# Row-by-row products of a matrix: GpSimd's early input batch moved behind the first load, and small loads added after the last store

## The chip, the cores and the metric

The kernel runs on one core of one Trainium2 chip. The metric is the device time of the launch in microseconds; lower is better.

## The reference

The input is a float32 matrix of 4096 rows and 256 columns. For each row the kernel must give all products of two of its elements, the upper triangle with the diagonal, 256 x 257 / 2 = 32,896 numbers a row:

```
dot = jnp.einsum('bi,bj->bij', inputs, inputs)
iu, ju = jnp.triu_indices(256)
return dot[:, iu, ju]
```

The input has 4.2 MB, the output 539 MB. There are no sums: one multiplication for each output element.

## The kernel before

**Tiling.** The 4096 rows are laid over 128 partitions, 32 rows each. A partition works on two rows at a time (REPEAT = 2), a group; sixteen groups make the kernel. The triangle of a group is cut into three pieces of about 10,960 columns (PIECES = 3), and each piece is built in one of two buffers in SBUF (`places`, printed as `o`), which are used in turn. As soon as a piece is built, SP stores it: 128 x 2 x 10,944 (or 11,008) float32, some 11 MB in one DMA. So there are 48 pieces, and the first of them goes out in five smaller stores (the columns in FIRST), so that the stream of stores begins early.

**Who multiplies.** In the loop each piece is shared by VectorE (DVE), which takes the longer runs of the triangle, and GpSimd (POOL), which takes the tail of the piece. Both read a copy of the group, `xv` in SBUF; DVE reads its other operand from `xp`, a copy in PSUM. The first two pieces are made ahead of the loop: piece 0 by DVE and ScalarE (ACT), reading the loaded input `x` itself until DVE has made `xp`, from the fourth part on (DIRECT = 3), and piece 1 (HELPED = 1) by DVE, ACT and GpSimd. GpSimd's share of piece 1 is the tail that an estimate in `tail` puts within HELP microseconds.

**Order.** The order is written out by hand with semaphores. `v_done`, `a_done` and `g_done` tell SP that the parts of a piece are there; `free` tells the engines that a buffer's store has landed; `go` passes that on from DVE to GpSimd. `head` counts the five stores of piece 0. `x_copied` tells DVE that GpSimd has made `xv`.

**Inputs.** SP loads three blocks at the start (NEAR): the first group, with the semaphore `loaded[0]`, then two more blocks. GpSimd issues the rest on its own queue in two batches: an early one (EARLY) at the start, and a late one (LATE) in the third pass of the loop (WHEN = 2). The early batch is a comb: COMB loads, each of every COMB-th row of partitions (`teeth` rows), then one of the `rest` rows. Between the loads stand small transfers, `mark`, that copy a few words of some rows into a buffer that nobody reads. The engines wait for all of these (`far`, `marked`) where they enter the loop.

**What the change touches.** The constants HELP, COMB and MARK; the main body where the early batch is issued (`mark(0, FORE)` and the loop after it) and where GpSimd waits for `loaded[0]`; the first product in `vector` that reads `xp`; the start of `gpsimd`; and the end of `sync`, after the last store. At its end SP takes back the semaphores that are still up: `x_read`, the three of `loaded`, and the two of `free`, which are up when the last stores have landed.

Of the kernel before, what the change touches and what calls it, by code (L numbers as in the profile page):

```python
# [8 lines left out]
F32 = mybir.dt.float32  # L9
# [3 lines left out]
P = 128  # L13
# [7 lines left out]
WHEN = 2  # L21
BEGUN, HAD = 2, 5
HELPED = 1
HELP = 15.0
COMB = 9
FORE, AFT = 5, 14
TENS, FIVES, SKIP = 100, 25, 2
MARK = 64
PLACES = 2
SETS = 5  # L30
PASS = 6
# [104 lines left out]
def kernel(  # L136
# [15 lines left out]
    nc = tc.nc  # L152
# [15 lines left out]
    edge = pool.tile([P, EDGE], F32, name="edge")  # L168
    places = [pool.tile([P, REPEAT, slot], F32, name=f"o{k}") for k in range(PLACES)]
    xt = pool.tile([P, passes, rounds * each], F32, name="x")  # L170
    xv = pool.tile([P, each + 1], F32, name="xv")
    marks = pool.tile([P, 2, 2 * MARK], F32, name="marks")

# [6 lines left out]
    free = [semaphore(f"free{k}") for k in range(PLACES)]  # L180
    head, v_done, a_done, go = (semaphore(s) for s in ("head", "v_done", "a_done", "go"))
    loaded = [semaphore(f"loaded{k}") for k in range(len(NEAR))]
    far, marked = semaphore("far"), semaphore("marked")
    teeth = P // COMB
    rest = P - COMB * teeth

# [38 lines left out]
    def vector(h, pieces: range, ahead: bool, done: int = 0) -> int:  # L225
        for p in pieces:
            place, copied = places[p % PLACES], None
            parts = blocks(p, ahead)
            if ahead and p == 0:
                for c, (_, _, _, block, lo) in enumerate(parts):  # L230
                    if c == DIRECT:
                        nc.vector.tensor_copy(xp, x_of(h, 0)).then_inc(v_own, 1)  # L232
                        done += 1
                        copied = done
                    for i, j, at, length in block:
                        ins = nc.vector.tensor_tensor(  # L236
                            place[:, :, at - lo : at - lo + length],
                            window(x_of(h, 0)[:, j:], [[d, REPEAT], [1, 1], [1, length]]),
                            window(xp[:, i:] if c >= DIRECT else x_of(h, 0)[:, i:], [[d, REPEAT], [1, 1], [0, length]]),
                            ALU.mult,  # L240
                        )
                        if copied:
                            ins._wait_ge(v_own, copied)
                            copied = None
                    ins.then_inc(v_done, 1)
                continue
            if ahead and p == HELPED:
                take(nc.vector, x_copied, 1)
            if not ahead and p % PIECES == 0:
                take(nc.vector, x_read, 1)  # L250
                for to in (xv[:, :each], xp):
                    ins = nc.vector.tensor_copy(to, x_of(h, p // PIECES))  # L252
                    if done:
                        ins._wait_ge(v_own, done)
                    ins.then_inc(v_own, 1)
                    done += 1
                copied = done
            if not ahead:
                if use(p) < uses:
                    nc.vector.wait_ge(free[p % PLACES], 16 * use(p)).then_inc(go, 1)  # L260
                else:
                    take(nc.vector, free[p % PLACES], 16 * uses)
                    nc.vector.sem_inc(go, 1)  # L263
            for _, _, _, block, lo in parts:
                order = interleave(block)

                own = (p + 1) % PIECES == 0 or p == pieces[-1]
                waits = schedule(order)
                counted = {*waits.values(), *([len(order) - 1] if own else [])}
                number = {k: done + 1 + c for c, k in enumerate(sorted(counted))}  # L270
                for k, ((i, j, at, length), m, _) in enumerate(order):
                    at -= lo
                    ins = nc.vector.tensor_tensor(  # L273
                        place[:, :, at : at + m * length],
                        window(xv[:, j:], [[d, REPEAT], [1, m], [1, length]]),
                        window(xp[:, i:], [[d, REPEAT], [1, m], [0, length]]),
                        ALU.mult,
                    )
                    if copied:
                        ins._wait_ge(v_own, copied)  # L280
                        copied = None
                    elif k in waits:
                        ins._wait_ge(v_own, number[waits[k]])
                    if k in counted:
                        ins.then_inc(v_own, 1)
                done += len(counted)
                if own:
                    nc.vector.wait_ge(v_own, done).then_inc(v_done, 1)
                else:
                    ins.then_inc(v_done, 1)  # L290
        return done
# [45 lines left out]
    def gpsimd(h, pieces: range, ahead: bool):  # L337

        done = turns = 0
        if ahead:  # L340
            nc.gpsimd.memset(xv[:, each:], 0.0).then_inc(g_own, 1)  # L341
            nc.gpsimd.tensor_copy(xv[:, :each], x_of(0, 0)).then_inc(g_own, 1)  # L342
            done += 2
            nc.gpsimd.wait_ge(g_own, done).then_inc(x_copied, 1)
        for p in [HELPED] if ahead else pieces:
            place = places[p % PLACES]
            block, lo = helped(p) if ahead else next((block, lo) for _, _, block, _, lo in blocks(p, False))
            turns += not ahead
            last = (p + 1) % PIECES == 0
            order = interleave(block)  # L350
            waits = schedule(order)
            counted = {*waits.values(), *([len(order) - 1] if last else [])}
            number = {k: done + 1 + c for c, k in enumerate(sorted(counted))}
            for k, ((i, j, at, length), m, _) in enumerate(order):
                at -= lo
                ins = nc.gpsimd.tensor_tensor(  # L356
                    place[:, :, at : at + m * length],
                    window(xv[:, j:], [[d, REPEAT], [1, m], [1, length]]),
                    window(xv[:, i:], [[d, REPEAT], [1, m], [0, length]]),
                    ALU.mult,  # L360
                )
                if k == 0 and not ahead:
                    ins._wait_ge(go, turns)
                elif k in waits:
                    ins._wait_ge(g_own, number[waits[k]])
                if k in counted:
                    ins.then_inc(g_own, 1)
            done += len(counted)
            if last:
                nc.gpsimd.wait_ge(g_own, done).then_inc(g_done, 1)  # L370
            else:
                ins.then_inc(g_done, 1)
            if p in (BEGUN, HAD) and not ahead:
                late(h, p)
            if last:
                nc.gpsimd.sem_inc(x_read, 1)
        nc.gpsimd.sem_inc(g_own, -done)
        if turns:
            nc.gpsimd.sem_inc(go, -turns)  # L379

    def sync():
        parts_done = done = joined = 0
        for turn in range(passes * PASS):
            h, p = divmod(turn, PASS)
            ahead, place = turn < AHEAD, places[p % PLACES]
            parts = list(blocks(p, ahead))
            if not ahead or p == HELPED:
                joined += 1
            for lo, hi, *_, base in parts:
                done += 1  # L390
                parts_done += ahead
                nc.sync.wait_ge(v_done, done)
                if ahead and p == HELPED:
                    nc.sync.wait_ge(g_done, joined)
                to = x_out[h, p // PIECES, :, :, base + lo : base + hi]
                store = nc.sync.dma_start(to, place[:, :, lo:hi])
                store._wait_ge(*((a_done, parts_done) if ahead else (g_done, joined)))
                store.then_inc(free[p % PLACES] if len(parts) == 1 else head, 16)
        for sem, count in ((v_done, done), (a_done, parts_done), (g_done, joined)):
            nc.sync.sem_inc(sem, -count)  # L400

# [32 lines left out]
    for engine in (nc.vector, nc.scalar):  # L434
        engine.wait_ge(loaded[0], 16)
    mark(0, FORE)
    for k in range(COMB + 1):
        load(EARLY, slice(k, k + COMB * (teeth - 1) + 1, COMB) if k < COMB else slice(P - rest, P))
        mark(FORE + rest * k, FORE + rest * k + (rest if k < COMB else AFT))
    nc.gpsimd.wait_ge(loaded[0], 16)  # L440

    take(nc.tensor, head, 16 * (len(FIRST) + 1))
    nc.tensor.sem_inc(free[0], 16)
# [2 lines left out]
        all_pieces(engine, pieces_of)  # L446
    sync()
    take(nc.sync, x_read, 1)
    for sem in loaded:
        take(nc.sync, sem, 16)  # L450
    for k in range(PLACES):
# [28 lines left out]
```

## Time and profile before

| what | value |
|---|---|
| time, median of 3 runs | 1263.46 us (1263.3 to 1263.96) |
| time of the profiled execution | 1263.19 us |
| its span in the profile | 1261.4 us |
| busy share of DVE, ACT, POOL | 63%, 2%, 64% |
| moved by DMA | 543.26 MB, mean 431 GB/s |
| share of the 16 DMA engines: SP's queue q1, GpSimd's queue q0 | 99.2%, 0.6% |
| stores of a whole piece, from issue to landing | 31.4 to 33.6 us |
| first products of DVE and ACT | 4.22 us |
| GpSimd's 21 early transfers issued | 1.61 to 13.60 us |
| GpSimd's products of piece 1 | 14.52 to 28.36 us |
| last store issued by SP | 1228.57 us |

The span runs from the first to the last instruction in the profile; the time of the same execution is 1.8 us longer. Times inside the profile count from the span's start. q1 and q0 are rings on the same sixteen DMA engines. The share of a queue is the time that its packets took, over the span of all sixteen.

### The profile page before, as it was taken

The page shows a single profiled execution, that of the slowest core. Times are in us where ns is not written, and L with a number is a line of the kernel's source. Part 1 is how long each engine was busy: PE and PEld are TensorE (multiplying, and loading weights), DVE is VectorE, ACT ScalarE, POOL GpSimd, SP SyncE. Part 2 cuts the span into 40 slices and gives each one's busy share as a digit, 9 for nine tenths or more (in the row PEclk, how much of TensorE's full clock was granted, in tenths as well). Part 3 has the DMA queues.
Part 4 walks back from the last instruction along what each step waited for, and adds up shares of the span by engine and source line. Part 5 has one row for each costly group of instructions (what it writes and reads, how often), then busy time and mean ns, then how long its engine had stood idle before and what let it go on. Part 6 is the DMA issues. An engine that isn't in the chain of part 4 may idle for free. (4 is left out here: it accounts for less than half of the span.)

```text
span 1261.4 us, 2947 instructions
## 1 busy us (share of the span) xinstructions
DVE 792.5 (63%) x1257; ACT 27.8 (2%) x76; POOL 805.0 (64%) x1134
## 2 busy tenths in 40 slices
DVE  8666747667474674766648666586655866468560
ACT  8000000000000000000000000000000000000000
POOL 8477665776566766577656775567656675576750
DMA  9999999999999999999999999999999999999998
GB/s 379 441 435 432 437 430 439 429 436 432 435 428 432 432 432 435 433 433 433 435 432 436 432 436 432 434 432 436 432 434 435 434 433 435 432 433 434 434 433 371
DMA packets 16136, 543.26 MB, mean 431 GB/s; under 512 B 1753, under 2 KB 1792, under 8 KB 3584
## 3 DMA queue, kind: packets, MB, share of 16 engines
q1 hardware_dynamic: 14704, 540.54, 99.2%
q0 software_dynamic: 1424, 2.65, 0.6%
q14 instruction: 8, 0.07, 0.0%
HBM read 4.21 MB, written 538.97 MB: 431 GB/s over the span
## 5 line engine op out<-in xcount | busy, mean ns | idle before, releaser
L356 POOL TENSOR_TENSOR o<-xv 128x52 f32<-128x52 f32 (+34 forms) x1103 | 789.5, 757 | 415.9 <-DVEq L260 282.2
L273 DVE TENSOR_TENSOR o<-xv,xp 128x356 f32<-128x356 f32 (+4 forms) x1196 | 759.7, 722 | 423.0 <-DMA out_dram<-o 301.3
L299 ACT ACTIVATE o<-x 128x198 f32<-128x198 f32 (+35 forms) x74 | 26.2, 463 | 1.4 <-DMA x<-in_r_inputs_dram 1.4
L252 DVE COPY xv<-x 128x512 f32 x15 | 6.4, 427 | 8.3 <-DVEq L188 8.3
L252 DVE COPY xp<-x 128x512 f32 x15 | 10.4, 695 | 0.5
L236 DVE TENSOR_TENSOR o<-x,xp 128x470 f32<-128x470 f32 (+18 forms) x19 | 9.7, 589 | 0.0
L323 POOL DMA_DIRECT2D x<-in_r_inputs_dram x13 | 7.7, 592 | 0.8 <-POOL o L356 0.8
L317 POOL DMA_DIRECT2D marks<-in_r_inputs_dram x12 | 7.0, 585 | 1.2 <-SPq L175 1.2
L236 DVE TENSOR_TENSOR o<-x 128x510 f32<-128x510 f32 (+9 forms) x10 | 5.7, 646 | 3.1 <-DMA x<-in_r_inputs_dram 3.1
L433 ACT ACT_TABLE_LOAD x1 | 1.3, 1283 | 1.2 <-ACTq L188 1.2
L431 DVE MEMSET edge<- 128x32 f32 x1 | 0.1, 85 | 1.0 <-SPq L175 1.0
L232 DVE COPY xp<-x 128x512 f32<-128x512 f32 x1 | 0.7, 687 | 0.0
L342 POOL COPY xv<-x 128x512 f32<-128x512 f32 x1 | 0.6, 623 | 0.0
L433 ACT ACTIVATE edge<-edge 128x1 f32<-128x1 f32 x1 | 0.3, 294 | 0.0
L467 POOL MEMSET const-float32-0.0<- 128x1 f32 x1 | 0.1, 100 | 0.2 <-issue 0.2
L341 POOL MEMSET xv<- 128x1 f32 x1 | 0.1, 118 | 0.0
L467 POOL MEMSET const-bfloat16-1.0<- 128x1 bf16 x1 | 0.1, 103 | 0.0
L467 POOL MEMSET const-uint8-127<- 128x1 uint8 x1 | 0.1, 103 | 0.0
L467 POOL MEMSET const-float32-1.0<- 128x1 f32 x1 | 0.1, 100 | 0.0
## 6 DMA issues: line engine op xcount, KB each, us to landing
out_dram<-o SPq DMA_DIRECT2D x31, 10944.0 KB, 33.6
out_dram<-o SPq DMA_DIRECT2D x16, 11008.0 KB, 31.4
out_dram<-o SPq DMA_DIRECT2D x1, 4352.0 KB, 17.0
out_dram<-o SPq DMA_DIRECT2D x1, 2624.0 KB, 12.7
out_dram<-o SPq DMA_DIRECT2D x1, 1984.0 KB, 10.8
out_dram<-o SPq DMA_DIRECT2D x1, 1280.0 KB, 7.5
x<-in_r_inputs_dram POOLq DMA_DIRECT2D x1, 1200.0 KB, 39.9
x<-in_r_inputs_dram SPq DMA_DIRECT2D x1, 1024.0 KB, 5.5
```

What stands on the lines that cost most here:

```text
L232: nc.vector.tensor_copy(xp, x_of(h, 0)).then_inc(v_own, 1)
L236: ins = nc.vector.tensor_tensor(place[:, :, at - lo : at - lo + length], window(x_of(h, 0)[:, j:], [[d, REPEAT], [1, 1], [1, length]]), wi ...
L252: ins = nc.vector.tensor_copy(to, x_of(h, p // PIECES))
L273: ins = nc.vector.tensor_tensor(place[:, :, at : at + m * length], window(xv[:, j:], [[d, REPEAT], [1, m], [1, length]]), window(xp[:, i:] ...
L299: nc.scalar.activation(places[p][:, r, at - lo : at - lo + length], xa[:, r * d + j : r * d + j + length], AF.Copy, scale=xa[:, r * d + i ...
L317: nc.gpsimd.dma_start(marks[lo:hi, :, :MARK], of).then_inc(marked, 16)
L323: nc.gpsimd.dma_start(to, of).then_inc(far, 16)
L341: nc.gpsimd.memset(xv[:, each:], 0.0).then_inc(g_own, 1)
L342: nc.gpsimd.tensor_copy(xv[:, :each], x_of(0, 0)).then_inc(g_own, 1)
L356: ins = nc.gpsimd.tensor_tensor(place[:, :, at : at + m * length], window(xv[:, j:], [[d, REPEAT], [1, m], [1, length]]), window(xv[:, i:] ...
L433: nc.scalar.activation(edge[:, :1], edge[:, 1:2], AF.Copy, scale=edge[:, 2:3])
L467: nc = _bacc.Bacc("TRN2", target_bir_lowering=False, num_devices=1)
```

## The change

- COMB goes from 9 to 3. The early batch becomes three loads of 42 rows and one of 2, in place of nine of 14 and one of 2. The marks between them fall from eleven to five.
- MARK goes from 64 to 16: a mark copies twice 16 words a row in place of twice 64.
- GpSimd's wait for `loaded[0]` moves from behind the early batch to ahead of it; the first mark stays ahead of the wait.
- HELP goes from 15 to 18: GpSimd takes a longer tail of piece 1.
- DVE's first product that reads `xp` now increments `go`, and GpSimd takes that before it sets up and copies `xv`.
- After the last store SP issues sixteen small loads, number k over k partitions with 2k words each, into a buffer `tiny` that nobody reads, with a semaphore `probed`. SP waits for all sixteen at the end, between `x_read` and `loaded`.

```diff
-HELP = 15.0
-COMB = 9
+HELP = 18.0
+COMB = 3
 FORE, AFT = 5, 14
 TENS, FIVES, SKIP = 100, 25, 2
-MARK = 64
+MARK = 16
...
+    tiny = pool.tile([P, 272], F32, name="tiny")
...
-    far, marked = semaphore("far"), semaphore("marked")
+    far, marked, probed = (semaphore(s) for s in ("far", "marked", "probed"))
...
                         if copied:
-                            ins._wait_ge(v_own, copied)
+                            ins._wait_ge(v_own, copied).then_inc(go, 1)
                             copied = None
...
         if ahead:
+            take(nc.gpsimd, go, 1)
             nc.gpsimd.memset(xv[:, each:], 0.0).then_inc(g_own, 1)
             nc.gpsimd.tensor_copy(xv[:, :each], x_of(0, 0)).then_inc(g_own, 1)
...
                 store.then_inc(free[p % PLACES] if len(parts) == 1 else head, 16)
+        at = 0
+        for k in range(1, 17):
+            nc.sync.dma_start(tiny[:k, at : at + 2 * k], x_in[:k, : 2 * k]).then_inc(probed, 16)
+            at += 2 * k
...
     mark(0, FORE)
+    nc.gpsimd.wait_ge(loaded[0], 16)
     for k in range(COMB + 1):
         load(EARLY, slice(k, k + COMB * (teeth - 1) + 1, COMB) if k < COMB else slice(P - rest, P))
         mark(FORE + rest * k, FORE + rest * k + (rest if k < COMB else AFT))
-    nc.gpsimd.wait_ge(loaded[0], 16)
...
     take(nc.sync, x_read, 1)
+    take(nc.sync, probed, 16 * 16)
     for sem in loaded:
         take(nc.sync, sem, 16)
```

## The prediction

> **What bounds the kernel now.** I read the page's slices first, then its queues, then the stretches at both ends.
>
> ```profile
> span 1261.4 us, 2947 instructions
> DVE 792.5 (63%) x1257; ACT 27.8 (2%) x76; POOL 805.0 (64%) x1134
> DMA  9999999999999999999999999999999999999998
> q1 hardware_dynamic: 14704, 540.54, 99.2%
> q0 software_dynamic: 1424, 2.65, 0.6%
> ```
>
> The reader is to see that no compute engine is busy for more than 64%, while the sixteen DMA engines are at nine tenths or more in every slice but the last. q1 (what SP issues: first loads and all stores) takes 99.2% of them, q0 (what GpSimd issues: later inputs and marks) 0.6%. 543.26 MB in 1261.4 us is 431 GB/s, 27 GB/s per DMA engine. So the time is: when the stream starts, plus the bytes of the slowest DMA engine, plus what follows the last landing.
>
> The start, by stretches (columns: stretch, its length, busy us of DVE, ACT and POOL, granted clock, DMA share, GB/s):
>
> ```profile
> 2.00:3.00 1.00, 0.00 (x0) 0.80 (x2) 1.00 (x3) 1.00 0.86 227
> 5.00:6.00 1.00, 1.00 (x3) 1.00 (x5) 1.00 (x3) 1.00 0.96 360
> 6.00:7.00 1.00, 1.00 (x3) 1.00 (x4) 1.00 (x3) 1.00 1.05 388
> 9.00:10.00 1.00, 1.00 (x3) 1.00 (x4) 1.00 (x3) 1.00 1.07 325
> 14.00:22.00 8.00, 8.00 (x16) 8.00 (x24) 7.74 (x8) 1.00 1.02 421
> ```
>
> From 2 us on the DMA engines are full; they only move less (small packets). Against 433 GB/s the stretches from 2 to 14 us lack some 770 KB, 1.8 us of work: that is all that a better start could give back.
>
> The end:
>
> ```profile
> 1208.00:1255.00 47.00, 20.11 (x41) 0.00 (x0) 14.74 (x39) 1.00 1.00 433
> 1256.00:1257.00 1.00, 0.00 (x0) 0.00 (x0) 0.00 (x0) 1.00 0.92 396
> 1258.00:1259.00 1.00, 0.00 (x0) 0.00 (x0) 0.00 (x0) 1.00 0.10 44
> ```
>
> Compute is over at 1228.5 us. The packets from 1258 on are nearly one engine's alone: among the last store's sixteen completion increments in the trace, two DMA engines end at 1255.9 to 1256.0 us, thirteen at 1257.7 to 1258.7, one at 1260.2. That one sets the end; SP's closing events then take 1.1 us to 1261.4.
>
> [...] The load of 100 rows took 39.9 us to land. [...]
>
> ```profile
> x<-in_r_inputs_dram POOLq DMA_DIRECT2D x1, 1200.0 KB, 39.9
> x<-in_r_inputs_dram POOLq DMA_DIRECT2D x9, 112.0 KB, 5.3
> ```
>
> [...] No view of before shows a tiny load behind a store[...].
>
> **The change, part by part.**
>
> *Early batch.* Nine loads of 14 rows become three of 42[...]. Marks shrink from 512 B to 128 B a row, and 12 of 21 early DMAs go. Each leaves about three records of 9 ns on each engine's q0: 12 x 27 ns = 0.3 us less, on the path.
>
> *The wait for the first load.* GpSimd issued loads from 2.34 us; now it waits until DVE's first product starts, 4.22 us. Behind the wait stand eight DMA issues: three loads at about 0.70 us (between 0.56 for 14 rows and 0.86 for 100), five small ones at 0.57: 4.9 us, done at 9.2 instead of 13.6 us. Their first data, about 4 us after issue (first mark issued 1.61, first q0 packet 5.68 us), comes at about 8.3 instead of 6.3 us. Who could run dry? q1 has the loads of SP until about 6.6 us (1.5 MB less the turns that q0 took) and the first store's packets from 6.68 us (issued at 5.48). q0 filled that seam with some 0.4 us of work per engine; I charge 0 to 0.5 us of idleness, 0.3. Later SP's stores are issued at 7.22, 10.01, 14.23, 20.31 and 30.88 us, while the ones ahead of them land at 10.7, 14.7, 20.9, 26.9 and 37.3: q1 doesn't dry even with q0 empty. The early rows are needed at 30.9 us, where DVE enters the loop[...]. Seam and saving cancel: start 0 us, bounds -1.0 (over half of the 1.8) to +0.7.
>
> *The wait for DVE and HELP 18.* GpSimd's memset, copy of x and products now stand behind the first product that reads xp: 10.57 + 0.65 = 11.2 us. With 0.93 us for memset and copy (13.59 to 14.52) the products begin at 12.2 instead of 14.52. They grow from 3527 to 4217 elements a row: 13.84 x 4217/3527 = 16.5 us, ending at 28.7 instead of 28.4. DVE's part (15 products, 10.61 us from 20.15) falls to 14 products and about 9.5 us, ending at 29.7; ACT's falls by two of 74. That store can be issued about 1.1 us earlier, but q1 is full until 37.3 us: 0.
>
> *Sixteen tiny loads.* SP issues them behind the last store (1228.57): 16 x 0.4 = 6.4 us, under the 25 us that this store still needs: 0. On the DMA engines they stand in ring order behind the store, so the late engine does them after 1259.8. It gets 1 to 16 of them, at 9 ns for the data and 9 for the increment: at most 0.3 us. A load's first access can be slow (the first 2 KB packets of the run took up to 0.59 us instead of 0.08): I take 0.5 us for all[...]. SP then finds five more waits after the tiny loads' one (first-load semaphores and both places), already met, 0.07 us each: 0.35. Tail +0.85[...].
>
> Sum on the profiled execution: 1263.19 us (span 1261.4 and 1.8 around it) + 0 + 0 + 0.85 = 1264.0. It is 0.27 us under the median 1263.46; from the median: **1264.3**. A measurement of this kernel can tell about 0.2%, 2.5 us, from no change.
>
> **Rivals.**
> 1. *The late engine gets more bytes.* [...] the DMA engine that ends 1.5 us after the others may take the nine early rows: 72 KB at 27 GB/s, 2.7 us, so 1267.0[...]. It decides from 1.7 us, six rows, on. [...] This is the case that ends slower.
> 2. *The tiny loads don't overlap.* Each takes its turn with a read of its own, 0.1 to 0.2 us: 1.6 to 3.2 us in place of the 0.5, so 1265.4 to 1267.0. For: reads behind a dry stream are new here. Against: q0's marks of 512 B take 27 ns each in the trace.
> 3. *The start gets better.* Fewer DMAs between the first stores give back 1.0 of the 1.8 us: 1263.3. For: the dip to 325 GB/s at 9 us, with q0 loads in it. Against: most of the lack is in SP's own 2 KB and 2.8 KB packets.
> 4. *It does not do what it says:* if the end doesn't wait for the tiny loads, only SP's 0.35 us stay: 1263.8.
>
> **The numbers.** Forecast 0.60 (1263.6 to 1265.8), rival 1 0.12, rival 2 0.13, rivals 3 and 4 0.15. Slower over 0.2% (above 1266.0): rival 1 nearly whole, most of rival 2 and a little of the forecast's upper edge, 0.24. Faster (below 1260.9) would need more than the whole start plus a rebalanced end: 0.04. Same: 0.72. The range 1262.9 to 1267.0 leaves out the rest of rival 1 and the best starts.
>
> **What would show it.** Right: the stretches from 14 us on unchanged, the last store landing within 1 us of 1260.2, tiny loads landing within 0.5 us of it, GpSimd's products from about 12.2 us, DVE's first wait at 38.97 within 1 us. Wrong: DMA share clearly under 1 between 6 and 9 us; a last stretch with more than one packet on the late engine; a tiny load landing over 1.5 us after the store.

## The result, and the profile after

The changed kernel takes 1265.22 us (median of 18 runs, 1264.95 to 1265.97) against 1263.46 us (18 runs). The ratio is 1.0015, 95% interval 1.0008 to 1.0021: 1.76 us slower, beyond the spread of the runs and under the 0.2% that the prediction sets as no change. The forecast was 1264.3, in 1262.9 to 1267.0. The profiled execution took 1265.15 us, with a span of 1263.4.

The totals of the page after:

```profile
span 1263.4 us, 2951 instructions
DVE 791.2 (63%) x1256; ACT 27.1 (2%) x74; POOL 801.2 (63%) x1124
DMA  9999999999999999999999999999999999999997
q1 hardware_dynamic: 14976, 540.56, 99.1%
q0 software_dynamic: 1136, 2.63, 0.6%
```

In the DMA row no slice but the last has another digit than before. The start, by the stretches shown of before (length, busy us of DVE, ACT and POOL, granted clock, DMA share, GB/s):

```profile
2.00:3.00 1.00, 0.00 (x0) 0.80 (x2) 0.34 (x1) 1.00 0.86 266
5.00:6.00 1.00, 1.00 (x3) 1.00 (x3) 1.00 (x3) 1.00 1.00 377
6.00:7.00 1.00, 1.00 (x3) 1.00 (x5) 1.00 (x3) 1.00 1.05 326
9.00:10.00 1.00, 0.97 (x3) 1.00 (x5) 0.00 (x0) 1.00 0.99 366
14.00:22.00 8.00, 8.00 (x14) 8.00 (x24) 8.00 (x8) 1.00 1.02 431
```

Early bytes come a little later (326 instead of 388 GB/s at 6 us) and are nearly made up by 22 us: summed over the stretches, 66 KB are still missing there, 0.15 us. The end:

```profile
1208.00:1255.00 47.00, 19.65 (x40) 0.00 (x0) 14.28 (x39) 1.00 1.00 433
1256.00:1257.00 1.00, 0.00 (x0) 0.00 (x0) 0.00 (x0) 1.00 0.76 311
1258.00:1259.00 1.00, 0.00 (x0) 0.00 (x0) 0.00 (x0) 1.00 0.06 5
1259.00:1260.00 1.00, 0.00 (x0) 0.00 (x0) 0.00 (x0) 1.00 0.02 1
```

From 1258 on there is hardly a byte. The last store lands earlier than before. In the trace a store's semaphore goes up sixteen times (752 times for the 47 whole stores), once for each DMA engine whose share has landed (a completion increment); the last of these comes at 1259.65 us instead of 1260.23. But the tiny loads' increments go on to 1261.86, the last ones 0.18 to 0.19 us apart, with every packet of the core already over at 1259.27. SP's own view shows both new costs, its DMA issues and then its wait (before, SP's waits of this kind were for stores; that line stands first):

```profile
1228.21 16.61 SPq L403 DMA_DIRECT2D tiny<-in_r_inputs_dram  x16
```

```profile
SPq L188 <- SPq L188: 30.9, 2, 26.0
SPq L189 <- SPq L189: 16.8, 1, 16.8
```

The issues took 16.6 us, 1.06 us each in the median, hidden under the store. The wait of 16.8 us (SP on a semaphore, summed, times, longest) ends at 1261.88 with the last tiny load; SP then steps through five waits that are already met and stands at 1262.21.

GpSimd and DVE at the start, from the order of time (start, duration, engine and line):

```profile
3.54 5.71 DVE L237 TENSOR_TENSOR o<-x 128x510 f32<-128x510 f32 x10 [2.42 <-DMA x<-in_r_inputs_dram]
3.81 0.63 POOL L324 DMA_DIRECT2D x<-in_r_inputs_dram  x1 [1.47 <-DMA x<-in_r_inputs_dram]
10.70 0.09 POOL L343 MEMSET xv<- 128x1 f32 x1 [2.16 <-POOLq L189]
11.62 16.44 POOL L358 TENSOR_TENSOR o<-xv 128x696 f32<-128x696 f32 x16 [0.26 <-POOL xv L344]
19.47 9.50 DVE L274 TENSOR_TENSOR o<-xv,xp 128x784 f32<-128x784 f32 x14
```

GpSimd is done issuing at 8.54 us, waits 2.16 us for DVE's first product from `xp`, and multiplies from 11.62.

### The profile page after: what moved, and what is told of

Read it like the earlier page. It is cut to its first block, busy times and chain, and to the rows that moved or that the text cites. A ratio compares the mean times of both kernels' runs of the same rounds, so it can differ in the third digit from the quotient of the medians.

```text
span 1263.4 us, 2951 instructions
## 1 busy us (share of the span) xinstructions
DVE 791.2 (63%) x1256; ACT 27.1 (2%) x74; POOL 801.2 (63%) x1124
## 5 line engine op out<-in xcount | busy, mean ns | idle before, releaser
L358 POOL TENSOR_TENSOR o<-xv 128x696 f32<-128x696 f32 (+33 forms) x1105 | 792.2, 758 | 415.3 <-DVEq L261 282.2
L274 DVE TENSOR_TENSOR o<-xv,xp 128x588 f32<-128x588 f32 (+4 forms) x1195 | 758.4, 712 | 424.2 <-DMA out_dram<-o 302.1
L300 ACT ACTIVATE o<-x 128x198 f32<-128x198 f32 (+34 forms) x72 | 25.5, 447 | 0.7 <-DMA x<-in_r_inputs_dram 0.7
L324 POOL DMA_DIRECT2D x<-in_r_inputs_dram x7 | 4.5, 647 | 2.3 <-DMA x<-in_r_inputs_dram 1.5
L318 POOL DMA_DIRECT2D marks<-in_r_inputs_dram x6 | 3.6, 603 | 1.2 <-SPq L176 1.2
## 6 DMA issues: line engine op xcount, KB each, us to landing
x<-in_r_inputs_dram POOLq DMA_DIRECT2D x1, 1200.0 KB, 40.3
```

Source lines behind the costliest of these rows:

```text
L274: ins = nc.vector.tensor_tensor(place[:, :, at : at + m * length], window(xv[:, j:], [[d, REPEAT], [1, m], [1, length]]), window(xp[:, i:] ...
L300: nc.scalar.activation(places[p][:, r, at - lo : at - lo + length], xa[:, r * d + j : r * d + j + length], AF.Copy, scale=xa[:, r * d + i ...
L318: nc.gpsimd.dma_start(marks[lo:hi, :, :MARK], of).then_inc(marked, 16)
L324: nc.gpsimd.dma_start(to, of).then_inc(far, 16)
L358: ins = nc.gpsimd.tensor_tensor(place[:, :, at : at + m * length], window(xv[:, j:], [[d, REPEAT], [1, m], [1, length]]), window(xv[:, i:] ...
```

## The experiments

Each was timed together with the kernel before, in three groups. Differences below are between medians of one group; before stood at 1263.55, 1263.59 and 1263.57 us. The 95% interval of a ratio is about 0.08% (1 us) wide on each side, wider than the scatter of the medians; where two experiments are compared, this holds for each.

**1. The change without its tiny loads.**

```diff
-            nc.sync.dma_start(tiny[:k, at : at + 2 * k], x_in[:k, : 2 * k]).then_inc(probed, 16)
...
-    take(nc.sync, probed, 16 * 16)
```

> The changed kernel without its sixteen tiny loads, their buffer and SP's wait for them; the rest of the change stays. Theory (the end costs 2.5 us: 12 increments on the late DMA engine at 0.18 us and 0.33 us of SP's waits; the new start gives back 0.6 to 0.7): about 1262.8 us, 0.7 below before, last store landing near 1259.6. Rival (the start is worth nothing, and the end costs only the measured 1.8): 1263.5. Second rival (the start costs, as the forecast's upper bound allowed): 1264.0 or more.

Measured 1262.45 us, 1.10 below before; ratio 0.9992 (0.9983 to 1.0000). So the end costs 1.76 + 1.10 = 2.86 us and the start gives back 1.10. Both sizes were larger than the theory had them. The second rival is out; the first (the start is worth nothing) only narrowly, since the interval ends at 1.0000; two kernels with the same or nearly the same start, COMB 3 with `go` and the loads on four engines (below), bear it out with 1.19 and 0.96 us under before. The profile of this kernel is of its slowest run (1263.40 us), with the last store landing at 1260.45 instead of the expected 1259.6. In each of the ten profiles in which a store's increment comes last, the run's time is 2.95 or 2.96 us more than that increment's; by that the last landing of the median run is estimated at 1259.5.

**2. The tiny loads alone on the kernel before.**

```diff
-MARK = 64
+MARK = 16
...
+            nc.sync.dma_start(tiny[:k, at : at + 2 * k], x_in[:k, : 2 * k]).then_inc(probed, 16)
...
+    take(nc.sync, probed, 16 * 16)
```

> The kernel before with the sixteen tiny loads alone (and MARK at 16[...]). Theory: 2.5 us more than before, about 1266.0, and more than the whole change; the last increments of the tiny loads 0.18 us apart over about 2.2 us after the last store. Rival (the tiny loads cost 1.8): 1265.2, like the whole change.

Measured 1266.41 us, 2.86 above before; ratio 1.0022 (1.0014 to 1.0031). It is the same 2.86 as between the change and experiment 1. In its trace the store's last increment comes at 1260.67 and the tiny loads' last twelve at 0.18 to 0.19 us spacing up to 1262.88: 2.21 us = 12 x 0.184. SP's five waits add 0.33 us after it. The sum, 2.54 us, is just the difference in what follows the store's last increment up to the run's time: 5.50 us here and in the change, 2.96 before. The remaining 0.3 us lie ahead of that increment, and half of them can be seen: in the three profiles with sixteen loads at the end, the late engine's last store packet takes 1.70 to 1.72 us instead of 1.63, and its increment follows after 0.54 to 0.56 us instead of 0.46 or 0.47. MARK at 16 is part of this kernel too; alone it came out 0.42 us under before, within noise (experiment 7).

**3. SP's wait for the tiny loads behind its other waits.**

```diff
     take(nc.sync, x_read, 1)
-    take(nc.sync, probed, 16 * 16)
...
         take(nc.sync, free[k], 16 * uses)
+    take(nc.sync, probed, 16 * 16)
```

> The changed kernel with SP's wait for the tiny loads moved behind all its other waits. Theory: the four or five waits that SP found behind it, 0.07 us each, are passed during the last store: 0.27 us less than the changed kernel, about 1264.9 to 1265.0. Rival (the waits run beside something else): no difference, 1265.2.

Measured 1265.05 us, 1.50 above before, where the change is 1.76 above: 0.26 us less. In its trace four waits of 0.07 us have moved to 1245.6 us and the fifth to 1259.73, all ahead of the tiny loads' last increment, and the run ends 0.33 us sooner after that increment. Place and size agree; the difference of the medians alone is within the intervals.

**4. The tiny loads ahead of the last store.**

```diff
+                if turn == passes * PASS - 2:
...
+                        nc.sync.dma_start(tiny[:k, at : at + 2 * k], x_in[:k, : 2 * k]).then_inc(probed, 16)
```

> The changed kernel with the sixteen tiny loads issued behind the last store but one, so that the last store's packets stand behind them on each DMA engine. Theory A (0.18 us is the time from one completion increment to the next when nothing else is left to do; it lies beside the packets of a store): the tiny loads cost 0 on the DMA engines, the time is that of the kernel without them plus at most 0.3 us, 1262.8 to 1263.2. Theory B (each tiny load holds its DMA engine for 0.18 us): the late engine still loses 12 x 0.18 = 2.2 us, 1265.0.

Measured 1264.11 us, 0.56 above before, 1.66 above experiment 1. Neither theory held: the tiny loads are not free under a store's packets, nor do they cost the full 2.2. The last store lands at 1260.94 us instead of the estimated 1259.5, and SP has only that one wait left. 1.66 us over the twelve loads of the late engine are 0.14 us each, three quarters of the 0.184. The trace alone gives nearly the same: from the last increment of the store ahead to that of the last store it has 27.47 us, before had 25.96, so 1.51 us or 0.13 a load. So most of it is time that the DMA engine loses, although its records show 9 to 13 ns.

**5. Four tiny loads, over four and over five partitions.**

```diff
-        for k in range(1, 17):
+        for k in [4] * 4:      # the other kernel: [5] * 4
-    take(nc.sync, probed, 16 * 16)
+    take(nc.sync, probed, 16 * 4)
```

> The changed kernel with four tiny loads of 4 partitions in place of the sixteen[...]. Theory (0.18 us a tiny load on each engine that it uses, and engine 4 ends last): 4 x 0.18 = 0.74 us lie on engines that end nearly a microsecond before the last one; only SP's waits remain, 0.2 to 0.4 above the kernel without tiny loads: 1262.6 to 1262.9. Rival (tiny loads cost by their number, wherever they go): a quarter of the 2.8 us, 1263.2.

> The changed kernel with four tiny loads of 5 partitions[...]. Theory: now the last engine has them too, 0.74 us and the way of one load more, 1263.4 to 1263.7, 0.7 above the run with 4 partitions. Rival (they cost by their number): the same as with 4 partitions.

Measured 1262.61 us on 4 partitions and 1263.52 on 5: 0.91 us for one more row in each of the four loads (and rows of 40 B instead of 32). On 4 partitions the tiny loads' last increment (1258.69) comes before the last store's (1259.79); on 5 the last four come at 1259.64, 1259.83, 1260.01 and 1260.20, after it (1259.46). So it is the fifth row that brings these loads onto the engine that ends last. The trace of the change fits. Its tiny packets stand in sixteen series, one for each DMA engine, each 2 or 3 ns behind the end of a packet of the last store. The load over k partitions is k packets of 8k B, in k of the series; the series begin with 8, 16, 24 and so on to 128 B, one each, so every load takes in the engines of the smaller ones. The series that ends last (1259.09 to 1259.27 us) begins with 40 B, the load over five partitions, and has the loads over five to sixteen, twelve in all. Counted from 0 in this order its engine is number 4. Each small load of SP's, data and increment together, costs it 0.13 to 0.18 us (the 0.13 and 0.14 of experiment 4 and the 0.184 between increments). Which of the two takes the time no run separates.

**6. The early batch placed otherwise.** Experiment 1 with three rows moved from the last early mark to the first:

```diff
-FORE, AFT = 5, 14
+FORE, AFT = 8, 11
```

> The changed kernel without tiny loads, with FORE at 8 and AFT at 11 instead of 5 and 14[...]. The bytes in total are the same. Theory (engine 4 alone sets the end): 2.7 us more than without the shift, about 1265.1, the last store landing near 1262. Rival (the end is set by the sum over all engines, or the late engine isn't number 4): no difference, 1262.5.

That this gives the late engine nine early rows was the author's estimate; the records do not name the engine of a packet. Measured 1263.83 us, 1.38 above experiment 1. The direction is that of the theory: the same bytes, placed otherwise, cost time, so the sum over the engines isn't what ends the kernel. The size is half. In the trace two engines now land the first whole store at 60.75 and 60.77 us, 1.9 ahead of the middle of the rest, and the last comes at 64.29 (in the change the first is alone at 61.24, the last at 63.59). The nine rows, if it was nine, are thus worth about 1.4 to 1.9 us rather than 2.7; why not the whole, no run shows. The end of this trace can't be compared with experiment 1's: the profile is of one of its fastest runs (1263.37 us, last landing at 1260.41, where about 1262 was expected), the other of experiment 1's slowest.

**7. The parts of the new start, each alone on the kernel before.** Their edits: the wait ahead of the batch; `COMB = 3`; HELP at 18 with the wait for `go`; `MARK = 16`; and `COMB = 3` with the wait for `go`.

> The kernel before with GpSimd's wait for the first load moved ahead of the early batch, nothing else. The kernel without tiny loads was 1.1 us faster than before; this asks which part gave it. Theory (fewer GpSimd transfers[...]): no gain here, 1263.3 to 1263.8. Rival (the first load lands at 3.5 instead of 4.2 us, and the whole stream starts earlier): 1262.5 to 1262.9, first products near 3.54 us.

> The kernel before with COMB at 3, nothing else: three loads of 42 rows in place of nine of 14. Theory (fewer GpSimd transfers): most of the 1.1 us, 1262.5 to 1262.9. Rival (the early landing of the first load): no gain, 1263.3 to 1263.8.

> The kernel before with HELP at 18 and GpSimd's wait for DVE's first product from xp, nothing else. All theories: the store of piece 1 is issued about a microsecond earlier or later into a full queue, no difference, 1263.3 to 1263.8. A gain of 0.3 us or more would put part of the better start on GpSimd's work beside DVE.

> The kernel before with MARK at 16, nothing else: marks of 128 B a row in place of 512. Theory: [...] at 27 ns for 512 B against some 13 ns: 0.1 to 0.2 us less, 1263.3 to 1263.5. Rival (the small marks are what gives the better start): 1262.5 to 1262.9.

> The kernel before with COMB at 3 and GpSimd's wait for DVE's first product from xp (HELP stays 15, the wait for the first load stays behind the batch). COMB at 3 alone was 2.1 us slower: GpSimd, done with its transfers at 7.04 us, multiplied beside DVE's ten products with two operands in SBUF, which took 1052 ns instead of 646. Theory (that collision is the whole loss): it goes, DVE's ten products are back at about 650 ns, and the time is at or under before, 1262.7 to 1263.4. Rival (loads of 42 rows themselves cost, in the queues): 1264.5 or more with DVE at 650 ns.

| kernel | median, us | to before, us | ratio, 95% interval |
|---|---|---|---|
| wait alone | 1263.34 | -0.25 | 0.9999 (0.9991 to 1.0007) |
| COMB 3 alone | 1265.69 | +2.10 | 1.0017 (1.0011 to 1.0024) |
| go and HELP 18 alone | 1263.41 | -0.18 | 0.9999 (0.9991 to 1.0007) |
| MARK 16 alone | 1263.17 | -0.42 | 0.9997 (0.9989 to 1.0006) |
| COMB 3 and go | 1262.38 | -1.19 | 0.9991 (0.9983 to 0.9999) |

Three parts alone are within noise. COMB 3 alone was a surprise for both theories: slower. DVE's and GpSimd's times tell why. First its group of ten early products on the page of before, then in the first 32 us of COMB 3 alone (busy us, mean ns, idle before):

```profile
L236 DVE TENSOR_TENSOR o<-x 128x510 f32<-128x510 f32 (+9 forms) x10 | 5.7, 646 | 3.1 <-DMA x<-in_r_inputs_dram 3.1
```

```profile
L236 DVE TENSOR_TENSOR o<-x 128x510 f32<-128x510 f32 (+9 forms) x10 | 9.8, 1052 | 2.8 <-DMA x<-in_r_inputs_dram 2.8
```

The mean hides which of them are slow. The eighth, before and in COMB 3 alone:

```profile
L236 DVE TENSOR_TENSOR o<-x 128x486 f32<-128x486 f32 x1 | 0.7, 660 | 0.0
```

```profile
L236 DVE TENSOR_TENSOR o<-x 128x486 f32<-128x486 f32 x1 | 1.8, 1776 | 0.0
```

In order of time, first GpSimd's copy before, then COMB 3 alone:

```profile
13.63 0.62 POOL L342 COPY xv<-x 128x512 f32<-128x512 f32 x1
```

```profile
3.87 9.80 DVE L236 TENSOR_TENSOR o<-x 128x510 f32<-128x510 f32 x10 [2.76 <-DMA x<-in_r_inputs_dram]
...
7.08 1.10 POOL L342 COPY xv<-x 128x512 f32<-128x512 f32 x1
8.45 15.20 POOL L356 TENSOR_TENSOR o<-xv 128x680 f32<-128x680 f32 x14 [0.26 <-POOL xv L342]
13.60 0.68 DVE L232 COPY xp<-x 128x512 f32<-128x512 f32 x1
```

Done with its fewer transfers at 7.04 us, GpSimd copies and multiplies while DVE still reads both operands from SBUF. DVE's products go from 646 to 1052 ns in the mean, GpSimd's copy from 0.62 to 1.10 us. The first four of the ten are as before; the last three, which stand wholly beside GpSimd's products, take 1.68 to 1.78 us instead of 0.64 to 0.66. So beside GpSimd's products those three, with both operands in SBUF, take 2.7 times as long. The control stands in the same trace: DVE's nineteen products with one operand in `xp`, beside the same work of GpSimd, take 587 ns, as before (589).

```profile
L236 DVE TENSOR_TENSOR o<-x,xp 128x470 f32<-128x470 f32 (+18 forms) x19 | 9.7, 587 | 0.0
```

With the wait for `go` the same loads start GpSimd's products after DVE has gone over to `xp`:

```profile
12.02 13.83 POOL L357 TENSOR_TENSOR o<-xv 128x680 f32<-128x680 f32 x14 [0.26 <-POOL xv L343]
```

```profile
L236 DVE TENSOR_TENSOR o<-x 128x510 f32<-128x510 f32 (+9 forms) x10 | 5.7, 647 | 2.8 <-DMA x<-in_r_inputs_dram 2.8
```

and the time falls by 3.3 us, to 1.19 under before. The pair differs in nothing but this wait, so GpSimd's early work is the cause; the durations show that it acts through the collision. How four late microseconds of DVE become 3.3 us of a kernel whose DMA engines stay nearly full, the traces show only in part. In COMB 3 alone DVE enters the loop late and its first piece there is late too:

```profile
41.52 20.11 DVE L273 TENSOR_TENSOR o<-xv,xp 128x260 f32<-128x260 f32 x41 [7.03 <-issue]
```

```profile
38.67 20.11 DVE L273 TENSOR_TENSOR o<-xv,xp 128x260 f32<-128x260 f32 x41 [8.20 <-PEq L444]
```

The second line is that of COMB 3 with `go`. The store of that piece is issued at 61.76 us instead of 58.91, hardly before the store ahead of it begins to land (62.57): DMA engines that were ahead are likely to find nothing to do (the shares of such short stretches don't settle it). At the next store's landing the sixteen increments lie within 0.95 us, with `go` within 2.3. The mean of the engines is late by only 0.3 us at that point; it is 1.5 late behind GpSimd's late batch (at 430 us), where store packets take up to 2.4 us instead of 1.62 in COMB 3 alone and none does in the other; and the last engine ends 3.4 us later. Whether the lost lead is what makes the late batch dearer was not tried.

So fewer, larger early loads together with the wait for `go` give the whole gain of the new start; the wait for the first load and HELP 18 add nothing that can be seen beside them. This kernel and experiment 1 are the fastest, by 0.1% and at the edge of what the intervals resolve; all 13 runs of COMB 3 with `go` (up to 1262.60) lie below all of before beside it (from 1262.95).

**Where the 1.1 us come from** was only narrowed down. The average engine shows little of it: the mean of the last store's sixteen increments is 1258.03 us before, 1257.97 after and 1257.92 with COMB 3 and `go`. The last increment moves: 1260.23, 1259.65, 1259.49 (and 1260.45 in experiment 1's slowest run).

The landings in between tell when, as far as one profile of each can. From the store that lands at 481 us, behind GpSimd's late batch, to the end, one of the sixteen increments can be followed as it moves from among the first three to the last place. Increments bear no engine's name; this one is followed by its steady drift. In every profile but that of experiment 4, with its tiny loads in between, it falls back by about the same, 4.1 to 4.4 us against the mean. What differs is its lead at 481 us: 2.0 us before and in experiment 1's profile, 2.7 in the change and with COMB 3 and `go`, 0.7 in COMB 3 alone (where the mean is late too, 482.7 us instead of 481.3). So the gain, and the loss of COMB 3 alone, is in place by then. At the last landing ahead of the late batch neither the mean increment shows the gain (347.46 us before, 347.63 after, 347.86 with COMB 3 and `go`) nor the last one (348.38, 348.63, 349.13); the place of the one engine isn't followed that far back.

Two accounts remain. One: q0 has 539 records of 4 or 8 B in the first 60 us before and 263 after, 17 fewer for each engine in the mean; twelve tiny loads of two records each cost the late engine 1.66 us under a store, 0.07 us a record, and 17 x 0.07 = 1.2 us, an estimate. But at 62 us the mean increment of the first whole store is later than before, 62.6 against 62.7 and 63.0, so the other engines must have paid it back (in COMB 3 with `go` the stretch from 8 to 9 us has 235 GB/s). The other: the late batch. Between 360 and 440 us some store packets take over 1.65 us; what they take beyond 1.62 is, per engine, 0.50 us before, 0.58 in experiment 1's profile, 0.27 after, 0.00 with COMB 3 and `go`, and 1.21 in COMB 3 alone. The lead at 481 us is small where this is large, in one profile each. That speaks for the second account; no run varied either alone, and it stays open.

## Why the prediction was right, and where not

**The verdict** (no change to be told from 0.2%, likelier slower than faster) and the range held. The point was 0.9 us low, and that it came out that near is luck: two terms were off with opposite signs, the tail by 2.0 us, the start by 1.1 and so just beyond its bounds (-1.0 to +0.7). One of the prediction's own signs of being wrong came true: the last tiny load lands 2.21 us after the store, where over 1.5 us was to speak against the prediction and under 0.5 for it. What happened at the end is rival 2, which had a chance of 0.13.

**Tail, forecast +0.85, measured +2.86.** The failed step is "9 ns for the data and 9 for the increment: at most 0.3 us". The duration of a packet's record was read as the time to the next. In the trace the increments of the late engine stand 0.184 us apart, 12 of them. Rival 2 (the tiny loads take turns) had the right price, 0.1 to 0.2 us a load: twelve in turn on one engine took 2.21 us. SP's five waits were sized right: 0.35 forecast, 0.33 in the trace, 0.26 us less in the medians of experiment 3. SP's issues were forecast at 0.4 us and took 1.06, 16.6 in all instead of 6.4; the cover named for them, 25 us, was wide enough.

**Early batch and first wait, forecast 0 (-1.0 to +0.7), measured -1.10 for the whole start.** That each engine has as many bytes as before was the author's estimate, and no trace shows which engine has which of GpSimd's rows. The load of 100 rows landed after 40.3 us (39.9 before). The seam was about right on the average (0.15 us missing by 22 us). The failed step is setting the saving (12 transfers of three records of 9 ns, 0.3 us) against the seam and charging 0: the seam is an average over the engines, which indeed hardly moved (1258.03 to 1257.97 us at the last store), while the end is one engine's, and that one gained. The three records were misread as well: the trace has 17 fewer for each engine in the mean, not 36. What sized the gain is open (above). Rival 3 (the start gives back 1.0) came true in size, and the part that it named, fewer transfers, is the one that gains (with `go`); but no bytes of the start's lack are back by 22 us, as it had it.

**The other timings.** GpSimd's wait was forecast to end at 4.22 us and ended at 3.81, since the first load landed at 3.5 us. That is no effect of the change: MARK 16 alone, with GpSimd's transfers from 2.3 us on as before, has it at 3.56, and COMB 3 alone at 3.85. From there the steps held: transfers done after 4.7 us (4.9 forecast), products from 11.62 (12.2), 16.44 us long (16.5), DVE's part 9.50 us (9.5), DVE's first wait over at 38.16 (38.97 within 1). No DMA share under 0.9 appeared between 6 and 9 us. The load of 42 rows took 0.62 us to issue (0.70 forecast).

**The wait for `go`** was priced at 0; alone with HELP 18 it came out 0.18 us under before, within noise. What the prediction did not see is what it protects: with early transfers that end at 7 us it is worth 3.3 us.

**Rival 1** (the late engine gets more bytes) did not occur: in the profile of the change the last store lands 0.58 us earlier than before, not 2.7 later. Experiment 6, meant to give the late engine nine rows, found 1.4 us where the rival had 2.7.

## What to carry to other kernels

When the DMA engines are the bound, keep a ledger for the one that ends last, not for the mean: four small loads cost 0.9 us more over five partitions than over four. Price a small transfer by the distance between completion increments (here 0.13 to 0.18 us on the engine that ends last), not by the length of its packets. And before GpSimd is freed early, look at what DVE reads at that time: a wait that seems to cost something may keep the two apart (here DVE's last three products with both operands in SBUF took 1.68 to 1.78 us beside GpSimd's instead of 0.64 to 0.66, and the wait was worth 3.3 us).

## What was not expected of the hardware

- A completion increment behind small loads came every 0.184 us on one DMA engine, with packet records of 9 to 13 ns.
- SP took 1.0 to 1.2 us to issue a load of 3 to 16 partitions with 24 to 128 B each (0.25 to 1.20 us for one or two partitions), 0.37 to 0.46 us for a transfer of 128 partitions.
- One DMA engine ended last in every profile, 0.5 to 2.3 us after the next; in the change the tiny loads mark it as the one that has the loads over five partitions and more.
- It falls back because its packets are stretched. Of some 7,650 store packets from 455 to 1229 us about 340 took longer than the usual 1.618 or 1.627 us, 4.0 to 4.2 us in all, in each of six profiles; hardly ever two at a time (at most five overlaps), so nearly all are on one engine. That is the 4.1 to 4.4 us of its way from the front to the last place. What stretches them no run shows.
